# Layer norm 1 of two batches on a host-transposed x instead of TensorE transposes, and fc's first differences on VectorE

## The chip, the core and the metric

The kernel runs on one core of one Trainium2 chip, in float32 throughout. The metric is the device time of one execution in microseconds; the time before is given below as the median of three runs. The engines are named as in the profile: PE is TensorE (PEld its weight loads), DVE is VectorE, ACT is ScalarE, POOL is GpSimd and SP is SyncE, which here only issues DMAs.

## The reference

One block of cross-attention with an MLP. Four batches of 512 rows (queries) by 512 features, an encoder sequence of 512 rows per batch, 16 heads of 32, an MLP of 2048:

```python
x = layer_norm(hidden_states, ln1_w, ln1_b)          # (x - mu) * rsqrt(var + eps) * w + b
q = heads(x @ q_w + q_b)
k = heads(encoder_hidden_states @ k_w + k_b)
v = heads(encoder_hidden_states @ v_w + v_b)
attn = softmax(where(mask, q @ k.T * scale, min))
hidden = merge(attn @ v) @ cproj_w + cproj_b + hidden_states
y = layer_norm(hidden, ln2_w, ln2_b)
y = gelu(y @ fc_w + fc_b, approximate=True)
out = hidden + y @ proj_w + proj_b
```

Layer norm 1 takes a mean and a variance per row of x, and a weight and an offset per feature.

## The kernel before, in words

The tiles are 128 partitions by 512. A *window* w (16 of them) is one batch with four heads; a *block* is half a window, 256 queries, so there are 32 blocks p = 2w + half. Of a block the scores are made on PE into the eight PSUM banks (`scores`, L260), DVE adds the mask and finds the minimum (`soften`, L266), ACT takes the exponential (L270), DVE transposes 32x32 squares into a buffer tb (`turn`, L278), and `copies` (L327 to L340) brings the squares to the partitions where they are wanted: four copies on POOL and twelve DMAs on SP, into a buffer pT (or, for some pairs, gt or xe). `attend` (L343) multiplies with v on PE some two or three blocks later (the table `due`, L1021) and DVE writes the result (oT, L362). pT is a single buffer, so the copies of the next pair start when `attend` of the pair before has given it back.

Beside the blocks run the other products. `put(p, ...)` (L960) lists by hand what is emitted in block p; `block` emits it at three places, `fill(0)`, `fill(1)` and `fill(2)`, and `run` takes items off the list by their cost in the first two (CHAIN is 3.4, a work item of 0.0 costs nothing). There is no scheduler behind this: every engine and the SP queue works in the order in which instructions are emitted. PSUM banks are handed out in a ring of eight by `acc_tile`.

Layer norm 1 before: `ln_stat` takes the statistics of 128 rows on DVE, `ln_rs` turns them into a factor on POOL, `ln_norm` normalizes rows (ACT for batches 1 and 2, DVE for the others), and `ln1_turn` (L189, through `ln_turn`, L153) transposes on PE, four 128x128 transposes per group of 128 features, so 16 per batch, and applies weight and offset while it takes the result out of PSUM into xT, a half of the buffer xe. `prep_q` (L212 and after) reads xT; `prep_k` and `prep_v` read eT, the transposed encoder rows, which the host has already transposed (`encT`). For batch 1 x is loaded into gt at the start (L896), the norm is in block 0 and the turns in block 4. For batch 3 x is loaded in block 12, the statistics are in blocks 13 and 15, the norm in 15 and the turns in 16 and 17.

The MLP of batches 0 and 1 also runs beside the blocks. Its first product (`fc_by_pair`, `fc_seven`) uses Strassen-Winograd sums, seven products in place of eight: the four differences of the normalized rows are made once per batch by `y_sums` (L489), the sums of weights by `fc_sums` (L551) on POOL. For batches 0 and 1 two of the four differences are on DVE and two on POOL. For batch 0 that is in block 11, ahead of the first fc product.

DMAs of weights (`load_w`, `load_mlp`), of the encoder rows (`load_enc`) and of residual rows (`load_h`) share the SP queue with the twelve DMAs of each `copies`.

Of the kernel before, what the change touches and what calls it, by code (L numbers as in the profile page):

```python
# [35 lines left out]
IN_G = (1, 3, 5, 7)  # L36
IN_XE = (25, 27, 29, 31)

BY_ACT = ((1, 1), (1, 2))
NORM_ACT = BY_ACT + ((2, 0), (2, 1))  # L40
MW = 8
WARM = 9
# [5 lines left out]


@with_exitstack  # L50
def xattn_block(ctx: ExitStack, tc: tile.TileContext, x, encT, mask, q_w, k_w, v_w, c_w, fc_w, p_w, vecs, rows, out):
    nc = tc.nc
    scale = float(np.float32(1.0) / np.sqrt(HD).astype(np.float32))

    def pools(stack, **bufs):
        return [stack.enter_context(tc.tile_pool(name=n, bufs=k)) for n, k in bufs.items()]

    const, keep, hids, tiles, small = pools(ctx, const=1, keep=1, hids=6, tiles=4, small=4)
    dram = ctx.enter_context(tc.tile_pool(name="dram", bufs=1, space=bass.MemoryType.DRAM))

    att = ctx.enter_context(ExitStack())
# [6 lines left out]
    row = const.tile([P, 3, D], F32, tag="row", name="row")  # L68
    m8 = one.tile([P, L], U8, tag="m8", name="m8")
    nhalf = const.tile([P, NT], F32, tag="nhalf", name="nhalf")  # L70
    qb = const.tile([P, NG], F32, tag="qb", name="qb")
    wc = one.tile([P, ND, D], F32, tag="wc", name="wc")

# [56 lines left out]
    def ln_rs(key):  # L130

        ve = small.tile([P, NT], F32, tag="ve", name=f"ve{key[0]}_{key[1]}")
        nc.gpsimd.tensor_scalar(ve, S["mv", key][:, :, 1], EPS, 1.0, ALU.add, ALU.mult)
        rs = small.tile([P, NT], F32, tag="rs", name=f"rs{key[0]}_{key[1]}")
        nc.gpsimd.tensor_tensor(rs, ve, nhalf, ALU.pow)
        S["rs", key] = rs
        if key in NORM_ACT:
            nm = small.tile([P, NT], F32, tag="nm", name=f"nm{key[0]}_{key[1]}")
            nc.gpsimd.tensor_tensor(nm, S["mv", key][:, :, 0], rs, ALU.mult)
            nc.gpsimd.tensor_scalar(nm, nm, -1.0, 0.0, ALU.mult, ALU.add)  # L140
            S["nm", key] = nm
# [27 lines left out]
    def load_enc(b):  # L169
        for d in range(ND):  # L170
            queue(b).dma_start(out=eT[:, d, :], in_=encT[b, ts(d, P), :])
# [6 lines left out]
    def ln1(b, part):  # L178

        xn = S["xn", b]  # L180
        for t in range(NT):
            if part == 2:
                ln_norm((1, b), t, xn[t], xn[t])
            elif t // 2 == part:
                ln_stat((1, b), t, xn[t])
        if part == 1:
            ln_rs((1, b))

    def ln1_turn(b, d):  # L189
        ln_turn((1, b), d, S["xn", b], xT)  # L190
# [71 lines left out]
    def soften(w, qt, *heads):  # L262
        for h in heads:
            s = score_tile()
            mn = small.tile([P, 1], F32, tag="mn", bufs=2 * HG, name=f"mn_{w}_{qt}_{h}")
            nc.vector.tensor_tensor_reduce(  # L266
                out=s, in0=S["sc", w, qt][h], in1=S["mb", w // NG], scale=1.0, scalar=FMAX,
                op0=ALU.add, op1=ALU.min, accum_out=mn,
            )
            nc.scalar.activation(s, s, AF.Exp, bias=mn, scale=-1.0, accum_out=S["sums", w][:, qt, h : h + 1])  # L270
            if h % 2:
                S["ps", w, qt, h // 2] = score_pair()
# [7 lines left out]
    def block(w, half, fill, pairs):  # L280

        q0, q1 = 2 * half, 2 * half + 1
        if half == 0:
            S["sums", w] = small.tile([P, NT, HG], F32, tag="sums", name=f"sums_{w}")
        tb = S["tb", w, half] = two.tile([P, NI, PW + 2 * HD], F32, tag="tb", name=f"tb_{w}_{half}")
        scores(w, q0)
        scores(w, q1)
        soften(w, q0, 0, 1, 2, 3)
        soften(w, q1, 0, 1)
        turn(w, q0, 0)  # L290
        turn(w, q0, 1)
        soften(w, q1, 2, 3)
# [9 lines left out]
        nc.vector.transpose(  # L302
            tb[:, :, PW:].rearrange("p j (a q) -> p a j q", a=2), rr.rearrange("p a h d -> p (a h d)")
        )
# [65 lines left out]
    def stays(b, t):  # L370

        return b == 0 or b == SPLIT and t < 2

    def load_h(b, *ts_):

        if ("xa", b) not in S:
            S["xa", b] = dram.tile([L, D], F32, tag=f"xa{b}", name=f"xa{b}")
        for t in ts_:
            if b == B - 1:

                S["h", b, t] = k_q(t // 2, t % 2)
            else:
                pool, tag = (hids, "hid") if stays(b, t) else (tiles, "xn")
                S["h", b, t] = pool.tile([P, D], F32, tag=tag, name=f"h_{b}_{t}")
# [103 lines left out]

    def y_sums(b):  # L489
        y11, y12, y21, y22 = y_blocks(b)  # L490
        e = nc.vector if b > SPLIT else nc.gpsimd
        sub(ys[:, 0], y12, y11)
        sub(ys[:, 1], y22, ys[:, 0])
        sub(y12, y22, y12, e)
        sub(ys[:, 2], y21, ys[:, 1], e)
# [348 lines left out]
    def do(fn):  # L844
        return [(0.0, fn)]

    def A(w):
        if w >= NW:
            return []
        return [  # L850
            (CHAIN, lambda: prep_k(w)),
            (CHAIN, lambda: prep_q(w)),
            (CHAIN, lambda: prep_v(w)),
        ]
# [4 lines left out]
    def turns1(b):  # L859
        return [(TURN, lambda d=d: ln1_turn(b, d)) for d in range(ND)]  # L860
# [19 lines left out]
    nc.scalar.dma_start(out=vec, in_=vecs)  # L880
    make_identity(nc, ident)
    nc.gpsimd.memset(nhalf, -0.5)
    load_enc(0)
    load_w(0, nc.sync, ("wv",))
    load_x(0)
# [15 lines left out]
    prep_v(0)  # L901
    prep_k(1)
    run(turns1(0))
    load_h(0, *range(NT))
    nc.sync.dma_start(out=wc, in_=c_w)
    load_mlp()
# [4 lines left out]
    ln_rs((1, 1))  # L911
    prep_q(0)
    v_bias(0)

    def norm1(b, *ts_):
        for t in ts_:
            S["xn", b][t] = tiles.tile([P, D], F32, tag="xn", name=f"xn1_{b}_{t}")
            ln_norm((1, b), t, S["xn", b][t], gt[:, ts(t, D)])

    S["xn", 1] = [None] * NT  # L920
    x3 = turns1(1)
# [24 lines left out]
    def pb_(b):  # L946
        return do(lambda: proj_bias(b))
# [7 lines left out]
    def norm(b, *ts_):  # L955
        return do(lambda: [norm2(b, t) for t in ts_])

    ahead, fills = {}, {}

    def put(p, *work, before=()):  # L960

        work = [item for part in work for item in part]
        ahead[p] = list(before)
        fills[p] = work

    k2, q2, v2 = A(2)
# [1 line left out]
    k4, q4, v4 = A(4)  # L968
    k5, q5, v5 = A(5)
    k6, q6, v6 = A(6)  # L970
    put(0, [(CHAIN, lambda: prep_v(1)), v2, k2], do(lambda: norm1(1, *range(NT))))
    put(1, [k3, (0.0, lambda: prep_q(1)), (CHAIN, lambda: (prep_v(3), load_enc(1)))])
    put(2, [q2], [k4])
    put(3, [q3, v4])
    put(4, [k5], x3, [v5])
    put(5, [q4, q5])
    put(6, [k6, q6])
    x1, x2, x3, x4 = inputs(2)
# [44 lines left out]
    for p in range(2 * NW):  # L1023
        w, half = divmod(p, 2)
        if half == 0 and w and w % NG == 0:
            make_mb(w // NG)
        run(ahead[p])
        for pair in due.get(p, ()):
            attend(*divmod(pair, 2))

        def fill(n, work=fills[p]):
            if n or not work or work[0][0] <= CHAIN:
                run(work, CHAIN if n < 2 else None)

        block(w, half, fill, any(cost > CHAIN for cost, _ in fills[p]))

    gelus()
    first_c = FIRST * FQ // 2
# [59 lines left out]
```

## Time and profile before

| | |
|---|---|
| time, median of 3 runs | 768.9 us (768.01 to 770.72) |
| the profiled execution | 768.29 us, its span 766.5 us |
| PE busy | 760.6 us (99% of the span) |
| DVE, ACT, POOL busy | 594.7, 337.1, 312.6 us |
| PE transposes, 128 in all (L158) | 1.9% of the chain that ended last |
| DMA | 131.44 MB, mean 171 GB/s |

Times in the lines of the timeline and of the chain are microseconds from the start of the span, then the duration. In the timeline a bracket at the end of a line tells how long the engine had been idle and what ended that. The chain follows back from the last instruction, at each step to what released it, so its pieces add up to the span. The PE spends the whole attention stage, to about 510 us, and the MLPs behind it without a visible gap; each piece of the chain is then a product by its line.

### The profile page before, as it was taken

The numbers are of one execution on the slowest core, as the hardware profiler recorded it, in microseconds if no ns is written. First come the engines' busy times: TensorE is split into PE (matmuls) and PEld (weight loads), VectorE is DVE, ScalarE is ACT, GpSimd is POOL, SyncE is SP. The second block draws the span as 40 slices with busy tenths as digits, with TensorE's granted clock in tenths as the row PEclk, the third lists the DMA queues.
The fourth block names the chain that finished last, engine by engine and source line by source line (L and its number), as shares of the span: only waits on it lengthen the run. The fifth ranks groups of instructions, "written<-read, shape, count | busy, mean of one in ns | idle before, by whom it ended". The sixth has DMA issues, their size and how long they took to land.

```text
span 766.5 us, 13025 instructions
## 1 busy us (share of the span) xinstructions
PE 760.6 (99%) x4474; PEld 520.1 (68%) x4474; DVE 594.7 (78%) x1188; ACT 337.1 (44%) x761; POOL 312.6 (41%) x330
## 2 busy tenths in 40 slices
PE   9999999999999999999999999999999999999998
PEld 7656555566754745565554566447888889988997
DVE  3889899878989757887888989855777886747862
ACT  2676766564776444737753567501202221021200
POOL 1525447369466374234575444530060014303152
PEclk9999999999999999999999999999999999999999
DMA  9978788466866766675656866793724412146001
GB/s 330 319 223 228 180 209 253 117 196 193 254 196 189 189 208 180 163 185 130 173 128 190 214 197 193 173 296 132 262 101 129 162 34 90 35 131 219 2 15 42
DMA packets 58721, 131.44 MB, mean 171 GB/s; under 512 B 10992, under 2 KB 16752, under 8 KB 58528
## 3 DMA queue, kind: packets, MB, share of 16 engines
q1 hardware_dynamic: 56592, 123.58, 56.2%
q0 software_dynamic: 1920, 7.01, 2.7%
q8 instruction: 36, 0.59, 0.3%
q14 instruction: 29, 0.24, 0.1%
q10 hardware_dynamic: 144, 0.02, 0.0%
HBM read 66.08 MB, written 11.01 MB: 101 GB/s over the span
## 4 chain that ended last, share of the span: by engine, by line
PE 98%; DVE 1%; POOL 0%; ACT 0%; issue 0%; POOLq 0%
PE q L518 25%; PE accp L578 11%; PE r L665 8%; PE sc L260 8%; PE av L357 8%; PE accq L229 7%; PE accc L397 7%; PE accv L240 7%; PE acck L217 7%; PE q4p L701 2%; PE q1p L719 2%; PE tp L158 2%; PE warm L891 1%; DVE ptt L266 0%; PE q3p L701 0%; PE q5p L701 0%
## 5 line engine op out<-in xcount | busy, mean ns | idle before, releaser
L270 ACT ACTIVATE ptt<-ptt,mn 128x512 f32<-128x512 f32 x256 | 181.6, 711 | 148.6 <-DVE mn L266 148.6
L266 DVE CUSTOM_DVE_ANT_0 ptt<-sc,mb 128x512 f32<-128x512 f32 x256 | 160.5, 682 | 19.2 <-PE sc L260 19.2
L278 DVE STREAM_TRANSPOSE tb<-ptt 128x1024 f32<-128x1024 f32 x128 | 153.5, 1217 | 0.3 <-ACT ptt L270 0.2
L335 POOL COPY pT<-tb 32x1088 f32<-32x1088 f32 x96 | 105.2, 1096 | 38.1 <-DVE oT L362 14.4
L578 PE MATMUL accp<-pbt,gt 128*128 128x512 f32 x192 | 84.9, 596 | 0.0
L518 PE MATMUL q<-yT,gt 128*128 128x256 f32 x320 | 78.9, 380 | 0.0
L539 ACT ACTIVATE ga<-ga,vec 128x512 f32<-128x512 f32 x40 | 26.7, 714 | 92.0 <-DVE ga L472 92.0
L578 PEld LDWEIGHTS accp<-pbt,gt 128*128 128x128 f32 x192 | 35.9, 190 | 45.8 <-issue 39.3
L518 PEld LDWEIGHTS q<-yT,gt 128*128 128x128 f32 x320 | 60.9, 190 | 8.6 <-DMA xa<-pbt 0.2
L260 PE MATMUL sc<-pbt 32*128 32x512 f32 x512 | 64.7, 614 | 0.0
L240 PEld LDWEIGHTS accv<-ptt,xe 128*128 128x128 f32 x512 | 59.1, 192 | 7.4 <-DVE mn L266 4.9
L518 PE MATMUL q<-ys,gt 128*128 128x256 f32 x240 | 61.6, 380 | 0.0
L240 PE MATMUL accv<-ptt,xe 128*128 128x128 f32 x512 | 60.0, 276 | 0.0
L217 PE MATMUL acck<-xe,ptt 128*128 128x512 f32 x128 | 58.9, 603 | 0.0
L229 PE MATMUL accq<-xe,ptt 128*128 128x512 f32 (+1 forms) x136 | 58.3, 574 | 0.0
L397 PE MATMUL accc<-wc,oT 128*128 128x512 f32 x128 | 56.4, 597 | 0.0
L472 DVE TENSOR_TENSOR ga<-q,ga 128x512 f32<-128x512 f32 (+1 forms) x60 | 36.2, 603 | 21.4 <-PE q L518 19.4
L518 PEld LDWEIGHTS q<-ys,gt 128*128 128x128 f32 x240 | 45.7, 190 | 6.1
L270 ACT ACTIVATION_READ_ACCUMULATOR ptt<-ptt,mn 128x1 f32 x256 | 47.8, 187 | 0.0
L252 POOL TENSOR_TENSOR v<-v,row 128x512 f32<-128x512 f32 x16 | 20.4, 1280 | 64.7 <-ACT v L245 64.3
L357 PE MATMUL av<-pT,v 128*32 128x256 f32 x768 | 46.4, 382 | 0.0
L229 PEld LDWEIGHTS accq<-xe,ptt 128*128 128x128 f32 x136 | 25.1, 190 | 30.7 <-issue 23.1
(181 smaller groups left out, 1163.4 us busy)
## 6 DMA issues: line engine op xcount, KB each, us to landing
pT<-tb SPq DMA_DIRECT2D x288, 136.0 KB, 2.4
pbt<-p_w_dram SPq DMA_DIRECT2D x40, 256.0 KB, 3.3
gt<-ws SPq DMA_DIRECT2D x20, 512.0 KB, 3.4
gt<-tb SPq DMA_DIRECT2D x48, 136.0 KB, 2.4
xe<-tb SPq DMA_DIRECT2D x48, 136.0 KB, 2.4
pbt<-fc_w_dram SPq DMA_DIRECT2D x24, 256.0 KB, 4.1
gt<-fc_w_dram SPq DMA_DIRECT2D x20, 256.0 KB, 3.4
ptt<-k_w_dram SPq DMA_DIRECT2D x16, 256.0 KB, 3.7
```

The lines of the kernel that those rows point to most:

```text
L217: nc.tensor.matmul(acc, S["wk", w][:, d, :], eT[:, d, :], start=(d == 0), stop=(d == ND - 1))
L229: nc.tensor.matmul(acc, S["wq", w][:, d, :], xT[:, d, c], start=(d == 0), stop=(d == ND - 1))
L240: nc.tensor.matmul(acc[:, ts(t, P)], eT[:, d, ts(t, P)], S["wv", w][:, d, :], start=(d == 0), stop=(d == ND - 1),)
L260: nc.tensor.matmul(S["sc", w, qt][h], qT[r, ts(qt, P)], kT[r, :], start=True, stop=True)
L266: nc.vector.tensor_tensor_reduce(out=s, in0=S["sc", w, qt][h], in1=S["mb", w // NG], scale=1.0, scalar=FMAX, op0=ALU.add, op1=ALU.min, acc ...
L270: nc.scalar.activation(s, s, AF.Exp, bias=mn, scale=-1.0, accum_out=S["sums", w][:, qt, h : h + 1])
L278: nc.vector.transpose(tv[:, qt % 2, 2 * k : 2 * k + 2], S["ps", w, qt, k])
L335: nc.gpsimd.tensor_copy(pT[ts(i, HD), i], tb[ts(i, HD), i])
L357: nc.tensor.matmul(av[ts(h, HD), : 2 * P].rearrange(shape, **kw), v[:, t, ts(h, HD)], p[t][h], start=(t == 0), stop=(t == NT - 1),)
L397: nc.tensor.matmul(acc, S["oT", b][:, g, ts(t, P)], wc[:, g, :], start=(g == 0), stop=(g == NG - 1))
L518: nc.tensor.matmul(o, x[:, k], y[:, k], start=(k == 0), stop=(k == 1))
L578: nc.tensor.matmul(acc, gT[q % 2][:, k, ts(t, P)], S["pw", b, q * FQ + k], start=(k == 0), stop=(k == FQ - 1))
```

## The change

The host passes x a second time, transposed (`rawT`). For batches 1 and 3 (`BY_ROW`) the turn on PE is gone:

- `ln_rs` writes the factor and the negated mean times the factor, per row, into a small tile rn; `store_rn` transposes it on DVE and stores it to DRAM with four small DMAs, `load_rn` reads it back as two tiles in which each of 128 partitions holds all 512 rows' values.
- `load_raw` loads the transposed x (four tiles), `ln1_rows` multiplies and adds on POOL, two operations per tile, eight per batch, and `ln1_affine` applies weight and offset per feature on ACT, four operations, straight into xT.
- The row-wise norms, four per batch, and the 16 PE transposes of each of the two batches with their way out of PSUM are gone.
- In batch 1 `load_raw` is at the start, right behind the turns of batch 0 and ahead of `load_h`, `store_rn` in block 0, `load_rn` in block 1 behind the encoder's rows of the next batch, `ln1_rows` in blocks 2 and 3, `ln1_affine` in block 4. In batch 3 the statistics are all in block 13, `load_raw` in 13, `store_rn` and `load_rn` in 14, `ln1_rows` in 16, `ln1_affine` in 17.
- The residual tiles of batch 1 that stay in SBUF use the two buffers (tag hid2) that the spread rows had; `load_h(1, 0, 1)` moves from block 16 to 17.
- `y_sums` of batch 0 is wholly on DVE and moves from the first fill of block 11 to a new place `mid`, in the middle of the block's `soften`; for batch 1 it is as before.

```diff
-BY_ACT = ((1, 1), (1, 2))
+BY_ROW = ((1, 1), (1, 3))
+BY_ACT = ((1, 2),)
...
-    const, keep, hids, tiles, small = pools(ctx, const=1, keep=1, hids=6, tiles=4, small=4)
+    const, keep, hids, tiles, small = pools(ctx, const=1, keep=1, hids=4, tiles=4, small=4)
...
+        if key in BY_ROW:
+            rs, nm = rn[:, :NT], rn[:, NT : 2 * NT]
+            nc.gpsimd.tensor_tensor(rs, ve, nhalf, ALU.pow)
+            nc.gpsimd.tensor_tensor(nm, S["mv", key][:, :, 0], rs, ALU.mult)
+            nc.gpsimd.tensor_scalar(nm, nm, -1.0, 0.0, ALU.mult, ALU.add)
+            return
...
+    def load_raw(b):
+        S["xn", b] = [tiles.tile([P, L], F32, tag="xn", name=f"raw_{b}_{d}") for d in range(ND)]
+        for d in range(ND):
+            nc.sync.dma_start(out=S["xn", b][d], in_=rawT[b, ts(d, P), :])
+
+    def store_rn(b):
+        nc.vector.transpose(rnT, rn)
+        d = S["rn", b] = dram.tile([2, L], F32, tag=f"rn{b}", name=f"rn{b}")
+        for i in range(NI):
+            nc.sync.dma_start(
+                out=d.rearrange("a (t i q) -> i (a t) q", i=NI, q=HD)[i], in_=rnT[i * HD : i * HD + 2 * NT, :]
+            )
+
+    def load_rn(b):
+        S["rows", b] = [hids.tile([P, L], F32, tag="hid2", bufs=2, name=f"rn_{b}_{i}") for i in range(2)]
+        for i in range(2):
+            nc.sync.dma_start(out=S["rows", b][i], in_=S["rn", b][i : i + 1, :].broadcast_to([P, L]))
+
+    def ln1_rows(b, *ds):
+        for d in ds:
+            for i, op in enumerate((ALU.mult, ALU.add)):
+                nc.gpsimd.tensor_tensor(S["xn", b][d], S["xn", b][d], S["rows", b][i], op)
+
+    def ln1_affine(b):
+        for d in range(ND):
+            nc.scalar.activation(
+                xT[:, d, :], S["xn", b][d], AF.Identity,
+                bias=vec[:, LN1B + d : LN1B + d + 1], scale=vec[:, LN1W + d : LN1W + d + 1],
+            )
...
         soften(w, q0, 0, 1, 2, 3)
+        run(mid)
         soften(w, q1, 0, 1)
...
-        e = nc.vector if b > SPLIT else nc.gpsimd
+        e = nc.gpsimd if b == SPLIT else nc.vector
...
+    def next_(fn):
+        return [(0.01, fn)]
...
     run(turns1(0))
+    load_raw(1)
     load_h(0, *range(NT))
...
-    put(0, [(CHAIN, lambda: prep_v(1)), v2, k2], do(lambda: norm1(1, *range(NT))))
-    put(1, [k3, (0.0, lambda: prep_q(1)), (CHAIN, lambda: (prep_v(3), load_enc(1)))])
-    put(2, [q2], [k4])
-    put(3, [q3, v4])
-    put(4, [k5], x3, [v5])
+    put(0, [(CHAIN, lambda: prep_v(1)), v2], do(lambda: store_rn(1)), [k2])
+    put(1, [k3, (0.0, lambda: prep_q(1)), (CHAIN, lambda: (prep_v(3), load_enc(1), load_rn(1)))])
+    put(2, [q2], [k4], do(lambda: ln1_rows(1, 0, 1)))
+    put(3, [q3, v4], do(lambda: ln1_rows(1, 2, 3)))
+    put(4, [k5, v5], do(lambda: ln1_affine(1)))
...
-    put(11, [k], do(lambda: y_sums(0)), [v], some(2), pb_(0))
+    put(11, [k, v], some(2), pb_(0), mid=do(lambda: y_sums(0)))
...
-    put(13, [k], some(2), [v], x2[:1])
-    put(14, [q], some(2))
-    put(15, some(2), x2[1:2], some(1), x2[2:], some(1))
+    put(13, [k], x2[:1], some(2), [v], x2[1:2], do(lambda: load_raw(3)))
+    put(14, do(lambda: store_rn(3)), [q], do(lambda: load_rn(3)), some(2))
+    put(15, some(4))
...
-    put(16, h_(1, 0, 1), [k, q], x3[:2], some(2), x3[2:3])
-    put(17, [v], x3[3:], h_(1, 2, 3), x4, cb(1), C(1))
+    put(16, do(lambda: ln1_rows(3, *range(ND))), [k, q], some(2))
+    put(17, h_(1, 0, 1), [v], next_(lambda: ln1_affine(3)), h_(1, 2, 3), x4, cb(1), C(1))
```

More of the change, by code (lines that the diff above doesn't have):

```diff
@@ L50, in xattn_block @@
 @with_exitstack
-def xattn_block(ctx: ExitStack, tc: tile.TileContext, x, encT, mask, q_w, k_w, v_w, c_w, fc_w, p_w, vecs, rows, out):
+def xattn_block(ctx: ExitStack, tc: tile.TileContext, x, rawT, encT, mask, q_w, k_w, v_w, c_w, fc_w, p_w, vecs, rows, out):
     nc = tc.nc
@@ L70, in xattn_block @@
     nhalf = const.tile([P, NT], F32, tag="nhalf", name="nhalf")
+    rn, rnT = (const.tile([P, HD], F32, tag=n, name=n) for n in ("rn", "rnT"))
     qb = const.tile([P, NG], F32, tag="qb", name="qb")
@@ L278, in turn, with block @@
         nc.vector.transpose(tv[:, qt % 2, 2 * k : 2 * k + 2], S["ps", w, qt, k])
-    def block(w, half, fill, pairs):
+    def block(w, half, fill, pairs, mid):
         q0, q1 = 2 * half, 2 * half + 1
@@ L382, in load_h @@
             else:
-                pool, tag = (hids, "hid") if stays(b, t) else (tiles, "xn")
-                S["h", b, t] = pool.tile([P, D], F32, tag=tag, name=f"h_{b}_{t}")
+                pool, tag, n = (tiles, "xn", 4) if not stays(b, t) else (hids, "hid2", 2) if b else (hids, "hid", 4)
+                S["h", b, t] = pool.tile([P, D], F32, tag=tag, bufs=n, name=f"h_{b}_{t}")
             Q[0].dma_start(out=S["h", b, t], in_=x[b, ts(t, P), :])
@@ L882, in xattn_block @@
     nc.gpsimd.memset(nhalf, -0.5)
+    nc.gpsimd.memset(rn, 0.0)
     load_enc(0)
@@ L913, in xattn_block @@
     v_bias(0)
[L915 to L921, printed above, removed]
     mlp = [
@@ L956, in norm, with put @@
         return do(lambda: [norm2(b, t) for t in ts_])
-    ahead, fills = {}, {}
-    def put(p, *work, before=()):
+    ahead, mids, fills = {}, {}, {}
+    def put(p, *work, before=(), mid=()):
         work = [item for part in work for item in part]
-        ahead[p] = list(before)
+        ahead[p], mids[p] = list(before), list(mid)
         fills[p] = work
@@ L1033, in fill @@
                 run(work, CHAIN if n < 2 else None)
-        block(w, half, fill, any(cost > CHAIN for cost, _ in fills[p]))
+        block(w, half, fill, any(cost > CHAIN for cost, _ in fills[p]), mids[p])
     gelus()
@@ L1074 @@
         "x": a["x"],
+        "rawT": np.ascontiguousarray(a["x"].transpose(0, 2, 1)),
         "encT": np.ascontiguousarray(a["ctx_2048"].transpose(0, 2, 1)),
```

## The prediction, made before the changed kernel ran

> **What bounds the kernel now.** I read the head of the page first, then the waits of the PE, then the chain of waits, which tells what a microsecond is worth in each place.
>
> ```profile
> span 766.5 us, 13025 instructions
> PE 760.6 (99%) x4474; PEld 520.1 (68%) x4474; DVE 594.7 (78%) x1188; ACT 337.1 (44%) x761; POOL 312.6 (41%) x330
> ```
> ```profile
> PE q L518 <- POOL yT L469: 1.1, 1, 1.1
> ```
>
> The PE is busy in 99% of the span, and beside the start the list of its waits holds this one alone: 1.1 us in block 11, for a difference that `y_sums` makes on POOL. So PE work that goes is time won, and work on another engine costs nothing until it makes the PE wait. The questions are how much PE work goes, whether that one wait goes, and which slack the moved work uses up.
>
> **What goes from the PE.** Rows of the chain, in order of time:
>
> ```profile
> 74.27 1.75 PE tp L158 x16
> ...
> 252.21 0.87 PE tp L158 x8
> 253.08 6.05 PE q L518 x28
> 259.13 0.44 PE tp L158 x4
> ...
> 267.13 0.44 PE tp L158 x4
> ```
>
> The turns of batch 1 are 1.75 us on the chain, those of batch 3 0.87 + 0.44 + 0.44 = 1.75. All four pieces lie between PE products that follow at once, so the whole is won: **-3.50**. Their way out of PSUM and the eight row-wise norms go from ACT and DVE, which nobody waits for there: 0.
>
> **The wait in block 11.** Its timeline, PE and DVE:
>
> ```profile
> 171.38 0.69 DVE L469 TENSOR_TENSOR ys<-yT 128x512 f32<-128x512 f32 x1
> ...
> 172.10 1.89 PE L518 MATMUL q<-yT,pbt 128*128 128x256 f32 x8
> 172.10 1.46 DVE L469 TENSOR_TENSOR ys<-yT,ys 128x512 f32<-128x512 f32 x1
> ...
> 175.84 0.40 DVE L302 STREAM_TRANSPOSE tb<-rr 128x256 f32<-128x256 f32 x1
> ...
> 179.58 1.94 PE L357 MATMUL av<-pT,v 128*32 128x256 f32 x32
> 181.44 1.14 PE L260 MATMUL sc<-pbt 32*128 32x512 f32 x8
> ```
> ```profile
> L335 POOL COPY pT<-tb x4: 1082/1278/1509, 169.3 to 173.1; 32x1088 f32<-32x1088 f32 x4
> L472 DVE TENSOR_TENSOR ga<-q,ga 128x512 f32<-128x512 f32 (+1 forms) x60 | 36.2, 603 | 21.4 <-PE q L518 19.4
> ```
>
> The fc product takes 179.58 - 172.10 = 7.48 us here and 6.05 undisturbed (the chain's row at 253.08). If all four differences are there in time, 1.43 go: **-1.43**. They will be: before, the first two stood behind two transposes and all eight `soften` and began at 171.38; now they stand ahead of both transposes and of four `soften`, and their input, turned in block 10, has long been there.
>
> The price is on DVE. Two differences took 0.69 + 1.46 = 2.15 there; four take 4 x 0.69 = 2.76 if nothing holds them up. So the block's last transpose, which ended at 176.24, ends 0.6 later, and behind it stand four additions of 0.6 that empty fc's PSUM banks. They end near 176.24 + 0.6 + 2.4 = 179.2. The PE's next scores begin at 181.44 - 1.43 = 180.0 and reach fc's banks with their fifth head, halfway through them, about 1 us later. Slack 1.8.
>
> Why did one difference take 1.46 and the other 0.69? In the same microseconds a POOL copy took 1.51 where another took 1.08: the two hold each other up, by 0.77 for the DVE. How many of the four will meet a POOL operation I take as in the row, every second one: 1.5 us, which the slack just covers: **+0.1**, bounds 0 (none) and 1.3 (all four wait 0.77: 3.1 against 1.8).
>
> The Trainium skill, "SBUF — State Buffer", section "Who interferes with whom", states that a DVE instruction with two SBUF inputs and a POOL instruction that reads SBUF shut each other out, the later one for the whole of the other. The two long rows agree. Since POOL has sums of weights and copies queued at that time, by this rule every one of the four would wait, and the term would be its bound of 1.3; the fast row, 0.69 among the same copies, is why I don't take it.
>
> **Rows on POOL, eight operations per batch.** Nearest rows: the same shape and engine, SBUF in and out.
>
> ```profile
> L368 POOL TENSOR_TENSOR h<-h,row x18: 1260/1274/1460, 114.3 to 388.7; 128x512 f32<-128x512 f32 x18
> 261.98 0.72 POOL L472 TENSOR_TENSOR wsum<-pbt 128x256 f32<-128x256 f32 x1 [12.93 <-DMA pbt<-fc_w_dram]
> 266.39 4.49 POOL L335 COPY pT<-tb 32x1088 f32<-32x1088 f32 x4
> 281.30 1.86 PE av L357 x32
> ```
>
> Eight at 1.27 are 10.2 us. In block 16 POOL sits idle for 12.93 us up to 261.98, and the eight fall into that hole. What follows, the sums of weights, the copies of pair 16 (done at 270.88, wanted at 281.30), the bias of v and four `c_bias`, keeps its place. In blocks 2 and 3 four operations each, 5.1 us, lie ahead of copies that are wanted two to three blocks later. Cost **0**; without that cover each microsecond would be one on the PE (rival 3). The spread rows (four small stores, two loads back, through DRAM) are asked for a block ahead of `ln1_rows` in batch 1, two ahead in batch 3; on SP the copies of later pairs wait behind that round trip, with blocks to spare: 0.
>
> **ACT.**
>
> ```profile
> 78.75 2.78 ACT L163 ACTIVATE xe<-tp,vec 128x512 f32<-128x512 f32 x4
> 83.38 7.06 PE accq L229 x16
> ```
>
> In batch 1 four operations stay four, in batch 3 they are four for two. Behind the copy of v they begin about 79.4 and end 2.8 later, at 82.2; the PE wants the first tile at 83.38 - 1.75 = 81.6 and the fourth 2.6 us after that, at 84.2. **0**. In block 17 the residual loads `h_(1, 2, 3)` wait on the SP queue for the first two of these operations, and the encoder's rows of batch 3 wait behind them; both are read a good part of a block later: 0.
>
> **The start.** `load_raw(1)` puts 1.05 MB ahead of the residual rows, cproj's and the MLP's weights, and so ahead of the first copies and of batch 1's encoder rows, which the PE wants next.
>
> ```profile
> 41.19 1.03 SPq L210 DMA_DIRECT2D ptt<-k_w_dram  x2
> 47.27 1.85 SPq L171 DMA_DIRECT2D xe<-encT_dram  x4
> 52.42 3.43 PE acck L217 x8
> ```
> ```profile
> L171 SPq DMA_DIRECT2D xe<-encT_dram x1: 431/431/431, 48.7 to 48.7; - x1
> DMA to landing us min/median/max: 5.2/5.2/5.2
> 40.00:45.00 5.00, 5.00 (x25) 3.21 (x24) 4.83 (x9) 4.51 (x12) 0.00 (x0) 1.00 0.75 212
> 45.00:50.00 5.00, 5.00 (x36) 3.25 (x35) 2.98 (x9) 2.42 (x6) 2.34 (x3) 1.00 0.45 154
> ```
>
> Four such loads are 1.85 us of issue and, at the 212 GB/s of the row, up to 5.0 of transfer; four small stores add little. SP has next to nothing to issue from 42.2 to 47.27, and from 40 to 50 the DMA engines are idle for 5 x (0.25 + 0.55) = 4.0 us. The delay ends there, but for 1 us at most. The last encoder tile lands at 48.7 + 5.2 = 53.9; the PE reads it as the fourth of four, at 52.42 + 2.6 = 55.0. Slack 1.1. **0**, upper bound 1.6.
>
> **Pair 13.** Here the slack is smallest: `load_raw(3)` stands on the SP queue just ahead of this pair's twelve DMAs.
>
> ```profile
> 212.60 8.20 SPq L340 DMA_DIRECT2D pT<-tb  x12
> 223.55 1.93 PE L357 MATMUL av<-pT,v 128*32 128x256 f32 x32
> ```
> ```profile
> L340 SPq DMA_DIRECT2D pT<-tb x1: 589/589/589, 220.2 to 220.2; - x1
> DMA to landing us min/median/max: 3.1/3.1/3.1
> 210.00:212.00 2.00, 2.00 (x38) 0.99 (x36) 0.19 (x2) 1.79 (x2) 1.60 (x3) 1.00 0.34 121
> 212.00:214.00 2.00, 2.00 (x20) 0.91 (x18) 1.32 (x4) 0.24 (x2) 1.62 (x3) 1.00 0.18 45
> 214.00:216.00 2.00, 2.00 (x5) 0.94 (x6) 2.00 (x7) 2.00 (x7) 1.98 (x4) 1.00 1.02 301
> ```
>
> The last of the twelve lands at 220.2 + 3.1 = 223.3 and the PE wants it at 223.55. The raw tiles go from about 210.5 (the last one behind DVE's last statistics, about 212), when the DMA engines are at 0.34 and 0.18, which leaves 2.7 us of their time; 1.05 MB at 301 GB/s are 3.5. About 0.8 spill into the copies' time, less the slack of 0.25: **+0.6**, bounds 0 and 3.2 (nothing of it hidden).
>
> **Sum.** -3.50 - 1.43 + 0.1 + 0.6 = -4.23. The profiled execution took 768.29 (span 766.5 and 1.8 around it), so 764.1. The median of the three runs is 768.9, 0.6 above the profiled one; I say **764.3**, between the two. With the terms at their good ends it is 768.29 - 4.93 = 763.4, with the first and second of them at their bad ends 768.29 - 4.93 + 1.3 + 1.1 = 765.8 (1.1 of pair 13).
>
> **Rivals.**
> 1. Pair 13 is late by the whole 1.05 MB: +3.2 in place of +0.6, **766.9**. For it: the DMA share of 1.02 right afterwards. Against: the free engines before.
> 2. The wait of block 11 moves rather than goes: all four differences wait for POOL, the scores of block 12 for DVE, +1.3 in place of +0.1, **765.5**. For it: 1.46 beside 0.69. Against: the 0.69. By the section of the Trainium skill named above it would be this one.
> 3. Slower: the row operations on POOL. They have 12.93 us of hole and 281.30 - 1.75 - 270.88 = 8.7 of slack behind it, so from 21.6 us for the eight, 2.7 each, `attend` of pair 16 waits. To end 2.3 above the time before they must take 21.6 + 4.2 + 2.3 = 28 us, 3.5 each; at 4 us each the stall is 10.4 and the time **774.6**. For it: POOL is named in the only wait, and no row shows a spread row as second input. Against: 1.27 in 18 rows, 1.46 at most.
> 4. The encoder's rows are late at 52.42 by the bound: +1.6, **765.9**.
>
> **How the numbers follow.** The forecast 0.62, rival 1 0.12, rival 2 0.10, rival 3 0.09, rival 4 0.07. About 0.3%, 2.3 us, is what a measurement of this kernel can tell from no change, so faster begins below 766.0: the forecast, rival 2 and most of rival 4, 0.78. Same: rival 1 and the rest of 4, 0.13. Slower: rival 3, 0.09. The range reaches from 762.9 (the good ends, and half a microsecond that a lighter DVE and ACT may win) to 767.2, over rivals 1, 2 and 4. The forecast's own is 763.4 to 765.8.
>
> **What would show it.** Right: no tp rows of batches 1 and 3, their neighbours on the chain touching; no PE wait for L469 and an fc product of 6.05 in block 11; row operations of 1.27 on POOL; the PE's av of pair 13 starting 0 to 1 us late, behind a DMA. Wrong: a PE wait for xT (the first accq of a batch behind ACT), for encoder rows at 52, for copies that stand behind `ln1_rows` on POOL, or scores behind DVE in block 12.

## The result and the profile after

The changed kernel takes 767.2 us (median of 17 runs, 765.15 to 769.48) against 768.9 us of the kernel before (17 runs, 767.78 to 770.72). The ratio is 0.9981, its interval 0.9973 to 0.9988: a gain of about 1.5 us, a third of the forecast 4.6, and 767.23 lies just outside the predicted range, which ended at 767.2. The profiled execution took 767.06 us.

The head of the page and, from the waits, the lines of the PE beside the start (total us, times, longest):

```profile
span 764.9 us, 13013 instructions
PE 758.5 (99%) x4442; PEld 516.5 (68%) x4442; DVE 591.0 (77%) x1186; ACT 336.0 (44%) x759; POOL 329.2 (43%) x347
```
```profile
PE av L396 <- DMA rn<-rnT: 1.3, 1, 1.3
PE av L396 <- POOL pT L374: 0.4, 1, 0.4
```

The one wait of before, in block 11, is gone, and two have come, both ahead of an `attend`. A third does not look like a wait: it lies inside a product. The chain shows all three (start, us, engine and product):

```profile
69.23 2.84 PE sc L298 x16
72.08 3.63 PE acck L255 x8
75.71 3.57 PE accv L278 x32
79.28 1.86 PE av L396 x32
...
172.00 6.05 PE q L557 x28
...
189.66 1.09 POOL pT L374
...
191.94 1.93 PE av L396 x32
...
222.26 1.60 DMA rn<-rnT
223.86 1.92 PE av L396 x32
...
252.49 6.04 PE q L557 x28
258.54 1.86 PE av L396 x32
```

What was forecast as won is there: k, v and av of block 4 touch without turns between them, fc's product of block 11 takes 6.05, and the one at 252.49 is followed by av at once. But the scores of block 4 take 2.84 us where they take 1.93 elsewhere, POOL's copies stand ahead of pair 11's av, and a DMA ahead of pair 13's.

**A ledger.** The PE is nearly always busy, so the start of one product on the chain, minus its start in the first profile of before, is the time won or lost up to that place. Between two columns the difference is what the stretch has won (negative) or given back. The columns are the first v, then av of the pairs 0, 2, 10, 11, 13 and 16, named by their place in before (v at 9.23; av at 55.85, 79.59, 179.65, 193.12, 223.62 and 281.30), and the end of the span (766.5). Ahead of av 56 lies the k product with the last encoder tiles of batch 1; ahead of av 80 the scores of block 4 and batch 1's turns; ahead of av 180 the fc product of block 11; ahead of av 193 and av 224 what the copies of pairs 11 and 13 cost; ahead of av 281 batch 3's turns.

| kernel | v | av 56 | av 80 | av 180 | av 193 | av 224 | av 281 | end |
|---|---|---|---|---|---|---|---|---|
| before, again | -0.2 | -0.2 | -0.2 | -0.2 | -0.2 | -0.2 | -0.2 | -0.1 |
| before, third | 0.6 | 0.6 | 0.6 | 0.6 | 0.6 | 0.6 | 0.6 | 0.6 |
| after | 0.5 | 0.5 | -0.3 | -1.6 | -1.2 | 0.2 | -1.5 | -1.6 |
| after, again | -0.5 | -0.5 | -2.2 | -3.5 | -3.1 | -2.0 | -3.7 | -3.8 |
| after, third | 0.0 | 0.3 | -1.5 | -2.8 | -2.4 | -1.2 | -2.9 | -3.1 |
| after, fourth | 0.5 | 2.6 | 2.3 | 1.0 | 1.4 | 2.0 | 0.3 | 0.1 |

Behind its start, every profile of before keeps the same distance to the first one. After wins the turns (1.75 us in block 4 where nothing is in the way, 1.7 behind av 224) and 1.3 in block 11, each time, and 0.15 behind av 281: 4.9 in all. It gives back 0.4 at pair 11 and 0.6 to 1.4 at pair 13 each time, and in some executions up to 2.1 at the start (v to av 56) and up to 1.4 in block 4. Over the four, the mean of what is given back is 0.6 up to av 56, 0.6 in block 4, 0.4 at pair 11 and 1.1 at pair 13: 2.7 of the 4.9, which leaves 2.2. (The first v is 0.1 late in the mean, but so it is in the three of before.) The spans agree: 764.4 in the mean of the four and 766.7 in the mean of the three, 2.3 apart.

The times are only 1.9 apart, 766.6 and 768.5, and the medians of all runs on the two chips 1.7 and 1.3. The rest lies outside the span, where no row of the profile shows it: the time minus the span is 1.7 to 1.9 us in every run of before that has a span on record, and 2.1 to 2.2 in every run of after, 0.35 more. The kernel of run 8 below does not have it (1.7 to 1.8), that of run 9 has (2.1 to 2.2), and neither has the rows of batches 1 and 3; so the rows are not needed for it, and its cause stays open.

In the rows that follow, nothing was lost.

In the timelines of after, the four differences on DVE (start, us, line, operation), and on POOL what ran beside them and, later, the eight row operations:

```profile
166.40 0.93 DVE L508 TENSOR_TENSOR ys<-yT 128x512 f32<-128x512 f32 x1
167.44 1.03 DVE L508 TENSOR_TENSOR ys<-yT,ys 128x512 f32<-128x512 f32 x1
168.39 0.68 DVE L508 TENSOR_TENSOR yT<-yT 128x512 f32<-128x512 f32 x1
168.99 0.68 DVE L508 TENSOR_TENSOR ys<-yT,ys 128x512 f32<-128x512 f32 x1
```
```profile
166.86 1.05 POOL L508 TENSOR_TENSOR wsum<-pbt,wsum 128x256 f32<-128x256 f32 x1
168.21 0.56 POOL L600 DMA_DIRECT2D ws<-wsum  x1 [0.30 <-POOL wsum L508]
168.77 0.54 POOL L601 DMA_DIRECT2D ws<-pbt  x1
...
248.67 10.37 POOL L218 TENSOR_TENSOR raw<-raw,rn 128x512 f32<-128x512 f32 x8
```

The eight take 10.37 us, 1.30 each, in POOL's idle stretch of block 16, and no PE wait stands near them. Of the four differences two take 0.25 and 0.35 longer than 0.68. They lie over POOL's sum at 166.86, itself 1.05 where such sums take 0.73; the two short ones begin where POOL only issues DMAs.

### The profile page after: what moved, and what is told of

Read it like the earlier page. It is cut to its first block, busy times and chain, and to the rows that moved or that the text cites. A ratio compares the mean times of both kernels' runs of the same rounds, so it can differ in the third digit from the quotient of the medians.

```text
span 764.9 us, 13013 instructions
## 1 busy us (share of the span) xinstructions
PE 758.5 (99%) x4442; PEld 516.5 (68%) x4442; DVE 591.0 (77%) x1186; ACT 336.0 (44%) x759; POOL 329.2 (43%) x347
## 4 chain that ended last, share of the span: by engine, by line
PE 98%; DVE 1%; POOL 0%; issue 0%; DMA 0%; SPq 0%; POOLq 0%
PE q L557 24%; PE accp L617 11%; PE sc L298 8%; PE r L704 8%; PE av L396 8%; PE accv L278 8%; PE acck L255 8%; PE accc L436 7%; PE accq L267 7%; PE q4p L740 2%; PE q1p L758 2%; PE tp L166 1%; DVE ptt L304 1%; PE warm L934 1%; PE q3p L740 0%; PE q7p L740 0%
```

## The experiments

Theories. A: the time is given back at three places that each have one cause, and a move of that one thing takes the loss away (block 4: `load_rn(1)` ahead of pair 1's DMAs; pair 11: POOL's order; pair 13: `load_raw(3)`). B: the raw tiles and rows load DMA and POOL as a whole, so that a wait moved at one place comes back at the next. Times are medians; "-" lines are after's unless said otherwise.

**1. `load_rn(1)` behind pair 1's DMAs.**

```diff
-    put(1, [k3, (0.0, lambda: prep_q(1)), (CHAIN, lambda: (prep_v(3), load_enc(1), load_rn(1)))])
+    put(1, [k3, (0.0, lambda: prep_q(1)), (CHAIN, lambda: (prep_v(3), load_enc(1)))], next_(lambda: load_rn(1)))
```

> The changed kernel, but the spread rows of batch 1 are loaded behind pair 1's twelve DMAs in block 1 instead of ahead of them. Theory (the scores of block 4 were late because DVE's first transposes of block 3 waited for the buffer tb, which pair 1's DMAs still read): those DMAs end about 1 to 2 us earlier, DVE's idle 1.26 us ahead of the transposes of block 3 and most of the 0.92 us on the PE in block 4 go: 0.5 to 0.9 us less than the changed kernel. Rival (the 1 MB of raw rows at the start is what makes DMAs late): the wait stays, no difference over 0.2 us.

767.09 us, 0.9979 (0.9969 to 0.9988). The SP queue and DVE in before with the scores of block 4 on its chain, then the same two in after (its scores are in the chain above), then all three in this kernel:

```profile
49.21 7.81 SPq L340 DMA_DIRECT2D gt<-tb  x12
62.48 2.37 DVE L278 STREAM_TRANSPOSE tb<-ptt 128x1024 f32<-128x1024 f32 x2
68.71 1.93 PE sc L260 x16
```
```profile
49.68 1.08 SPq L213 DMA_DIRECT2D rn<-rn  x2
50.87 9.48 SPq L379 DMA_DIRECT2D gt<-tb  x12
...
64.34 2.37 DVE L316 STREAM_TRANSPOSE tb<-ptt 128x1024 f32<-128x1024 f32 x2 [1.26 <-ACT ptt L308]
```
```profile
51.25 7.80 SPq L379 DMA_DIRECT2D gt<-tb  x12
...
63.78 2.37 DVE L316 STREAM_TRANSPOSE tb<-ptt 128x1024 f32<-128x1024 f32 x2
```
```profile
70.02 1.93 PE sc L298 x16
```

In before the issue of pair 1's twelve DMAs began at 49.21 and took 7.81, to 57.02, which is 1.2 us behind av of pair 0 (55.85). In after it ends at 60.35, 4.0 behind (56.37), here at 59.05, 1.9 behind (57.16). Of after's twelve the last was issued at 59.8, and with their median of 4.1 us to landing that is 63.9. They read tb, which has two buffers, and the transposes at 64.34 write the same one again: DVE stands idle for 1.26 us, and the PE's scores of block 4 wait inside for banks that DVE has not emptied. With `load_rn(1)` behind, DVE doesn't stand idle, the scores take 1.93, and the stretch from av 56 to av 80 wins its whole 1.75 (1.31 to -0.44). The timeline names ACT as the releaser, though ACT's exponentials for these four heads had ended by 62.99 and DVE's idle time began only at 63.08: the name is of the semaphore that came last by the record, not of the cause.

One profile would not show this, since two of after's four lose nothing here either. But all five profiles with this move (runs 1, 4, 5, 6 and 14) win the whole 1.75 in block 4, and of the seven without it (after's four, runs 2, 3 and 7) five lose 0.85 to 1.4. The time does not show it: 0.5 to 0.9 less than after was expected, and the ratio is that of after. In this profile pair 13 gave back 2.3 and the start 1.4; what the other runs gave back there is not on record. A holds at this place by the profiles.

**2. `load_raw(3)` out of pair 13's way.**

```diff
-    put(13, [k], x2[:1], some(2), [v], x2[1:2], do(lambda: load_raw(3)))
+    put(13, [k], x2[:1], some(2), [v], x2[1:2])
-    put(15, some(4))
+    put(15, do(lambda: load_raw(3)), some(4))
```

> The changed kernel, but the raw rows of batch 3 are loaded in block 15 instead of 13; the four small stores stay in block 14. Theory (pair 13's DMAs stood behind 1 MB of raw rows): the PE's wait of 1.33 us ahead of pair 13 goes, 1.0 to 1.4 us less than the changed kernel unless pair 14 waits next (its copies on POOL ended 1.0 us before they were wanted). Rival (the small stores hold the semaphore or the queue, as the named releaser says): the wait of 1.3 us stays.

765.14 us, 0.9953 (0.9939 to 0.9967). The SP queue of after around pair 13's DMAs, then this kernel's, then its chain:

```profile
209.50 2.60 SPq L200 DMA_DIRECT2D raw<-rawT_dram  x4
212.22 9.47 SPq L379 DMA_DIRECT2D pT<-tb  x12
221.79 1.43 SPq L206 DMA_DIRECT2D rn<-rnT  x4
```
```profile
212.25 8.43 SPq L379 DMA_DIRECT2D pT<-tb  x12
220.79 1.45 SPq L206 DMA_DIRECT2D rn<-rnT  x4
```
```profile
217.23 6.04 PE q L557 x28
223.27 1.86 PE av L396 x32
```

The PE's av of pair 13 follows fc's product at once. Without the raw tiles the twelve are issued in 8.43 us in place of 9.47 (8.20 before), the last at 220.1 in place of 221.1, and their median way to landing is 3.3 us in place of 3.9, the longest 4.2 in place of 6.2. The small stores rn<-rnT, which the waits of after name, are still there: they stand behind the twelve on the queue and only land last. Nothing came back at block 14 or later (-0.35 at av 224, -2.11 at av 281, which is batch 3's turns). A holds again. The median is 2.1 us below after's, where the profiles of after show 1.1 for this place; the difference is not explained.

**3. The bias of the residual rows behind pair 11's copies.**

```diff
-    put(11, [k, v], some(2), pb_(0), mid=do(lambda: y_sums(0)))
+    put(11, [k, v], some(2), mid=do(lambda: y_sums(0)))
-    put(13, [k], x2[:1], some(2), [v], x2[1:2], do(lambda: load_raw(3)))
+    put(13, pb_(0), [k], x2[:1], some(2), [v], x2[1:2], do(lambda: load_raw(3)))
```

> The changed kernel, but the four POOL additions of proj's bias (5.0 us) move from block 11 to the start of block 13. Theory (pair 11's copies on POOL stand behind them and end 0.4 us late): the PE's 0.43 us of waiting for POOL's copy goes, 0.4 to 0.5 us less than the changed kernel. Rival (pair 11's DMAs are late as well): the wait stays, with a DMA as its releaser.

766.82 us, 0.9976 (0.9965 to 0.9987). POOL in before, in after and here:

```profile
187.65 4.47 POOL L335 COPY pT<-tb 32x1088 f32<-32x1088 f32 x4
```
```profile
176.82 1.27 POOL L290 TENSOR_TENSOR v<-v,row 128x512 f32<-128x512 f32 x1 [2.81 <-ACT v L283]
...
182.50 4.96 POOL L407 TENSOR_TENSOR h<-h,row 128x512 f32<-128x512 f32 x4
187.41 4.47 POOL L374 COPY pT<-tb 32x1088 f32<-32x1088 f32 x4
```
```profile
183.06 4.49 POOL L374 COPY pT<-tb 32x1088 f32<-32x1088 f32 x4
```

In before the copies of pair 11 ended at 192.12 and the PE wanted them at 193.05. After moves the PE up by 1.3 and POOL by 0.25 only. POOL has lost its two differences (2 x 1.27), but now stands idle for 2.81 us until ACT has copied v:

```profile
175.15 0.58 ACT L245 COPY v<-accv 128x512 f32<-128x512 f32 x1
```
```profile
173.80 0.72 ACT L308 ACTIVATE ptt<-ptt,mn 128x512 f32<-128x512 f32 x1 [1.97 <-DVE mn L304]
...
176.09 0.58 ACT L283 COPY v<-accv 128x512 f32<-128x512 f32 x1
```

The first row is before's, the others after's: the copy of v is 0.94 later, since ACT's exponentials ahead of it wait for DVE's `soften`, which the four differences in `mid` push back. So the copies end at 191.88, the PE's av starts at 191.94, and 0.4 of the 1.3 is gone again. With the bias behind, the copies end at 187.6 and the wait is gone (-0.99 at av 180, at av 193 and at av 210). It is gone in all five profiles with this move (runs 3, 4, 5, 6 and 14), and 0.4 stands there in all seven of after and its variants without it. A holds for the third time, and the loss belongs to the differences, not to the rows; run 8 shows it alone. The time cannot tell 0.4 us: the intervals of 0.9976 here and 0.9981 for after overlap.

**4 and 5. The three moves together.** Run 1's and run 3's edits, with `load_raw(3)` and `load_rn(3)` both in block 15 (run 2's move, and the loads of the rows with it). Run 5 is the same kernel once more, beside runs of after on the same chip.

```diff
-    put(13, [k], x2[:1], some(2), [v], x2[1:2], do(lambda: load_raw(3)))
-    put(14, do(lambda: store_rn(3)), [q], do(lambda: load_rn(3)), some(2))
-    put(15, some(4))
+    put(13, pb_(0), [k], x2[:1], some(2), [v], x2[1:2])
+    put(14, do(lambda: store_rn(3)), [q], some(2))
+    put(15, do(lambda: (load_raw(3), load_rn(3))), some(4))
```

> All three moves in one, and the spread rows of batch 3 loaded in block 15 too. Theory (three separate waits of 0.92, 0.43 and 1.33 us, each of one cause): together 2.0 to 2.7 us less than the changed kernel, about 764.5 us in the runs' median, 4.4 less than before. Rival (a new wait takes each place): no more than 1.2 us less than the changed kernel.

> The kernel with all three moves once more, beside the changed kernel on the same chip. Theory (three waits, one cause each): 1.5 to 2.5 us less than the changed kernel in the runs' median. Rival: less than 1 us.

765.42 us, 0.9963 (0.9950 to 0.9977), and again 765.09 us, 0.9952 (0.9940 to 0.9963), beside 767.63 of after on that chip: 2.5 us less than after, where 1.5 to 2.5 was expected. The chain of the second one:

```profile
48.01 7.47 DMA xe<-encT_dram
...
221.50 1.93 PE av L396 x32
```

| kernel | v | av 56 | av 80 | av 180 | av 193 | av 224 | av 281 | end |
|---|---|---|---|---|---|---|---|---|
| run 4 | 0.1 | 1.4 | -0.4 | -1.7 | -1.7 | -1.7 | -3.4 | -3.6 |
| run 5 | -0.7 | 0.8 | -1.0 | -2.2 | -2.2 | -2.1 | -3.8 | -4.0 |
| run 1 | -0.1 | 1.3 | -0.4 | -1.7 | -1.3 | 1.0 | -0.7 | -0.9 |
| run 2 | 0.7 | 1.3 | 0.4 | -0.8 | -0.4 | -0.4 | -2.1 | -2.3 |
| run 3 | -0.1 | 1.1 | 0.3 | -1.0 | -1.0 | 0.1 | -1.6 | -1.8 |

Behind av 56 the three moves win everything that was forecast as won: 1.75, 1.3, 0, 0.0 to 0.1 lost at pair 13, 1.7. In these two executions nothing has come back elsewhere, against B; runs 6 and 14, which hold the three moves too, do show new waits. What is left is the stretch ahead of av 56, the product with the last encoder tiles of batch 1: 1.2 and 1.5 given back in these two. In run 5 the wait has the name of the encoder's rows themselves. In run 4 it has that of DVE, but the first of the four tiles was issued at 47.75 and landed 5.4 us later, at 53.15, and the product began at 53.23.

By time alone the sum of the three is less clear than by the profiles: run 2, with one of the moves, took 765.14 on the chip on which run 4 took 765.42, six runs each.

**6 and 7. The MLP's weights out of the start.** They stand on the queue between the raw tiles and the encoder's rows; run 6 moves them in run 4's kernel, run 7 in after's.

```diff
-    load_mlp()
-    put(7, [v6, k], cb(0))
+    put(7, [v6, k], cb(0), do(load_mlp))
```

> The kernel with all three moves, and the first 2 MB of MLP weights loaded in block 7 instead of at the start. Theory (batch 1's encoder rows land late at 53 us because the raw rows are one load too many for the DMA engines of the first 50 us): the PE's 0.7 us of waiting ahead of k of block 2, and the 1.2 us that this stretch lost in all, go; 1.0 to 1.3 us less than with the three moves alone, 4.6 less than before. Rival (the wait is for DVE, as the named releaser says): it stays.

> The changed kernel with nothing but the first 2 MB of MLP weights moved to block 7. Theory (a full DMA queue at the start makes both the encoder rows and pair 1's DMAs late): no wait ahead of k in block 2, and the 0.92 us of block 4 go as well, though the spread rows are still loaded ahead of pair 1's DMAs; pair 11 and pair 13 keep theirs: 0.9 to 1.5 us less than the changed kernel. Rival (the place of the spread rows alone holds up pair 1's DMAs): block 4 keeps its 0.9 us.

765.41 us, 0.9962 (0.9950 to 0.9974), and 767.12 us, 0.9978 (0.9967 to 0.9989): no gain over run 4 and after, where about 1 us was expected. Ahead of av 56 the two give back 0.4 and 0.1, less than most others, but run 6 has a new wait at pair 13. Its POOL, PE and weight loads:

```profile
210.18 0.73 POOL L511 TENSOR_TENSOR wsum<-pbt 128x256 f32<-128x256 f32 x1 [7.47 <-DMA pbt<-fc_w_dram]
...
217.93 4.47 POOL L374 COPY pT<-tb 32x1088 f32<-32x1088 f32 x4
```
```profile
222.45 1.93 PE L396 MATMUL av<-pT,v 128*32 128x256 f32 x32 [1.62 <-DMA ptt<-q_w_dram]
```
```profile
222.45 1.45 PEld L396 LDWEIGHTS av<-pT,v 128*32 128x32 f32 x32 [2.02 <-POOL pT L374]
```

POOL's sums wait for weights until 210.18, its copies of pair 13 end at 222.40, and the PE starts at 222.45. The matmuls' row names a DMA, but the weight loads of the same product name the copy. In run 7 block 4 still gave back 1.4, as it may with `load_rn(1)` where it was (the rival's forecast), pair 13 1.85, and 0.5 came at a place of block 8.

**8 and 9. The differences alone.** Run 8 is before with the differences on DVE in `mid`, without the rows; run 9 is before with the first two lines of this edit only: on DVE, where they were.

```diff
-        e = nc.vector if b > SPLIT else nc.gpsimd
+        e = nc.gpsimd if b == SPLIT else nc.vector
...
+        run(mid)
...
-    put(11, [k], do(lambda: y_sums(0)), [v], some(2), pb_(0))
+    put(11, [k, v], some(2), pb_(0), mid=do(lambda: y_sums(0)))
```

> The kernel before with the second part of the change alone: all four differences of batch 0 on VectorE, in the middle of block 11's row minima. Theory: the fc product of block 11 takes 6.05 us instead of 7.48, and pair 11's copies on POOL, which follow ACT's later copy of v, take back 0.4 to 0.5 at the start of block 13: 0.9 to 1.0 us less than before. Rival (the late copies of pair 11 come from the raw rows' part): the whole 1.43 us stay won.

> The kernel before with all four differences on VectorE at their old place, behind all row minima of block 11. Theory (the engine was the matter, not the place): VectorE's four take 2.8 to 4 us from 171.4, the last ends at 174.2 to 175.4, ahead of the product that reads it; the fc product takes 6.05 to 6.4 us, and ACT's copy of v is late by as much as with the new place, so 0.6 to 1.2 us less than before. Rival (the place is what does it): the fc product still waits 0.5 us or more.

768.13 us, 0.9986 (0.9977 to 0.9995), and 769.11 us, 1.0005 (0.9997 to 1.0014). The chain of run 8, and then POOL and the weight loads of av in run 9:

```profile
190.94 1.09 POOL pT L336
```
```profile
188.01 4.47 POOL L335 COPY pT<-tb 32x1088 f32<-32x1088 f32 x4
```
```profile
192.53 1.45 PEld L357 LDWEIGHTS av<-pT,v 128*32 128x32 f32 x32 [1.18 <-POOL pT L335]
```

| kernel | v | av 56 | av 80 | av 180 | av 193 | av 224 | av 281 | end |
|---|---|---|---|---|---|---|---|---|
| run 6 | -0.4 | 0.1 | -1.7 | -2.8 | -2.8 | -1.2 | -2.9 | -3.0 |
| run 7 | 0.5 | 0.6 | 0.2 | -0.5 | -0.1 | 1.7 | 0.0 | -0.1 |
| run 8 | 0.4 | 1.0 | 1.0 | -0.3 | 0.1 | 0.2 | 0.2 | 0.2 |
| run 9 | -0.6 | -0.5 | -0.5 | -1.4 | -0.6 | -0.5 | -0.5 | -0.5 |

Run 8 has no rows, wins 1.34 in block 11 and gives 0.4 back at pair 11 as after does. So that loss is the differences' own. In run 9 the engine alone wins 0.8, and pair 11 takes all of it: POOL's copies end at 192.48, av starts at 192.53. A gain of 0.6 to 1.2 was expected of run 9, and none came: the median of its eleven spans is 766.9, as in before on that chip, and the time outside the span is 0.35 longer. (That its profiled span ends 0.5 early is the start's, -0.6 at the first v.) What the differences' new place wins over the old one is 0.5 in fc's product and 0.35 at pair 11. Run 8 also gave back 0.66 ahead of av 56, without a raw tile or a row in it.

**10 to 13. Before and after, two more profiles of each.** No edit.

> The kernel before, unchanged, for a second profile. Theory (k of block 2 waits for encoder rows in every kernel of this family, by as much as the DMAs happen to be late, and the changed kernel's raw rows add to it): a wait ahead of k in block 2 of 0 to 0.7 us, none in block 4, none at pairs 11 and 13. Rival (the wait belongs to the raw rows alone): none.

> The kernel before, unchanged, for a third profile; as with the second: 0 to 0.7 us ahead of k in block 2 by the theory, none by the rival.

> The changed kernel, unchanged, for a second profile. Theory: waits of 0.8 to 1.0 us in block 4, 0.4 to 0.5 at pair 11 and 1.1 to 2.3 at pair 13 in every execution, and 0.5 to 1.4 us ahead of k in block 2 whenever the first k of the kernel is not late. Rival (the first profile was a chance): one or more of the four is missing.

> The changed kernel, unchanged, for a third profile; as with the second: waits in block 4, at pair 11 and at pair 13 by the theory, one or more of them missing by the rival.

768.12, 768.99, 764.83 and 765.58 us. They are the rows of the first ledger: pairs 11 and 13 give back in every profile of after, the stretch ahead of av 56 and block 4 in some. Before gives back nothing at any of the four places, so the theory that it too waits ahead of av 56 is not borne out.

**14 and 15. The raw tiles of batch 1 behind pair 1's DMAs, and after once more.** Run 14 is run 4's kernel without raw tiles at the start; the eight row operations move to block 3.

```diff
-    load_raw(1)
-    put(1, [k3, (0.0, lambda: prep_q(1)), (CHAIN, lambda: (prep_v(3), load_enc(1)))], next_(lambda: load_rn(1)))
-    put(2, [q2], [k4], do(lambda: ln1_rows(1, 0, 1)))
-    put(3, [q3, v4], do(lambda: ln1_rows(1, 2, 3)))
+    put(1, [k3, (0.0, lambda: prep_q(1)), (CHAIN, lambda: (prep_v(3), load_enc(1)))],
+        next_(lambda: (load_raw(1), load_rn(1))))
+    put(2, [q2], [k4])
+    put(3, do(lambda: ln1_rows(1, 0, 1, 2, 3)), [q3, v4])
```

> The kernel with all three moves, and the raw rows of batch 1 loaded behind pair 1's DMAs in block 1, together with the spread rows; all eight POOL operations of batch 1 in block 3. Theory (the raw rows at the start make batch 1's encoder rows late): no wait ahead of k in block 2 beyond what the kernel before has, 0.4 to 1.2 us less than with the three moves alone. Rival (that wait is the DMA's scatter and not the raw rows): as long as with the three moves alone, within 0.3 us.

> The changed kernel once more, on the same chip as the two others. Theory: 0.2 to 0.3% less than before, with the waits at pair 11 (0.5 us) and pair 13 (1.1 to 1.4 us) and, in some executions, in block 4 (0.9).

765.32 us, 0.9951 (0.9938 to 0.9964), no different from run 5's 765.09 on the same chip, and 767.63 us, 0.9983 (0.9971 to 0.9995), for after. The first line is from run 14's waits of the PE; then DVE and the chain, and then the weight loads of pair 13's av:

```profile
PE acck L255 <- DMA xe<-encT_dram: 1.6, 2, 0.9
```
```profile
76.64 2.37 DVE L316 STREAM_TRANSPOSE tb<-ptt 128x1024 f32<-128x1024 f32 x2 [0.77 <-DMA pT<-tb]
...
82.02 2.35 PE sc L298 x15
```
```profile
223.82 1.24 PEld L396 LDWEIGHTS av<-pT,v 128*32 128x32 f32 x28 [0.65 <-POOL pT L374]
```

| kernel | v | av 56 | av 80 | av 180 | av 193 | av 224 | av 281 | end |
|---|---|---|---|---|---|---|---|---|
| run 14 | 0.6 | 2.3 | 0.6 | -0.3 | -0.3 | 0.2 | -1.5 | -1.6 |

It gives back 1.7 ahead of av 56 without a raw tile on the queue before it; the fourth profile of after gave back 2.1 with them. So the raw tiles at the start are not shown to be the cause. The weight loads show that the product waits for the encoder's tiles: for 3.1 us here, 1.4 in the fourth of after, 2.3 in run 8, and not at all in the three of before and in run 9. Why these tiles land late stays open; nine of the twelve profiles with rows give back 0.3 or more there.

Two more waits are new here. The raw tiles and the rows now stand ahead of pair 2's DMAs, DVE stands idle for them at 76.64, the DMAs' own name beside it, and the scores of the next block take 2.35: run 1's loss, one pair later. And POOL, whose sums waited for weights until 211.54, ends its copies of pair 13 at 223.77, with 0.5 lost, as in run 6. So A holds for its three places, but B is not refuted: these two profiles show that a load moved to another place can make a wait there.

## Why the prediction was wrong, by its steps

- **Turns, -3.50: right.** 1.75 in block 4 where nothing is in the way, 1.7 in blocks 16 and 17 in all profiles.
- **Block 11, -1.43: right in mechanism**, 1.3 in the ledger, the product 6.05. **The hold-up, +0.1:** nothing was lost: two of four were held up as assumed, but by 0.25 and 0.35 rather than 0.77 each, and no scores stood behind DVE in block 12. The Trainium skill, "SBUF — State Buffer", section "Who interferes with whom", fits these rows better than the prediction had it: the two differences that met a POOL sum on SBUF were long, the two beside POOL's DMA issues were not. The error was to take a POOL with work queued for a POOL that computes all the time. The fast row of before, 0.69, was also misread as an exception: it began at 171.38, ahead of the POOL copy that began at 171.5, and that copy was the one with 1.51; the difference behind it began during the copy and took 1.46. The later one paid each time.
- **The step that is missing at pair 11: failed, +0.4.** The prediction followed the later DVE only to fc's banks. It also delays `soften`, so ACT's exponentials, so ACT's copy of v, which POOL needs before it comes to pair 11's copies; and these had 0.93 us to spare before, less than the 1.3 by which the PE moved up in block 11. Runs 3 and 8 show it.
- **"On SP the copies of later pairs wait behind that round trip, with blocks to spare: 0": failed, +0.6.** It asked when pT is wanted by the PE and forgot who waits for tb to be read: two buffers, so the pair after next waits on DVE, and behind it the PE's scores. Run 1 shows it for `load_rn(1)`. It is not in every execution of after.
- **Pair 13, +0.6: mis-sized.** 0.6 to 1.4 in four profiles, 1.1 in the mean, 2.3 in run 1; the mechanism is right (run 2). The bound of 3.2 held; the slack of 0.25 and the bytes alone did not give the size, since the landing of the twelve also got longer.
- **The start, 0 with a bound of 1.6: mis-sized.** 0.6 up to av 56 in the mean, 2.1 once, over the bound. Rival 4's place was right; that the raw tiles cause it is not shown, since run 14 has the wait without them.
- **"Span 766.5 and 1.8 around it": failed, +0.35.** The sum kept the 1.8 for the changed kernel without a reason, and it is 2.1 to 2.2. Why stays open.
- **Rows on POOL, 0, and ACT, 0: right.** 10.37 us in the idle stretch against 10.2, no wait. Rival 3 fell, and so did rival 2, since no scores of block 12 waited.

In sum: 4.9 won as forecast; 2.7 given back inside the span and 0.35 outside it, where the forecast had 0.7. Of the 2.3 missed, 1.35 (0.4, 0.6 and 0.35) are three steps with no price, and most of the rest is two prices too low, the start by 0.6 and pair 13 by about 0.5. That 767.23 nearly touches the range is chance: its upper end stood for rivals 1, 2 and 4, and none of them came as it was priced.

## What to carry to other kernels

On a kernel whose main engine is never idle, a microsecond won there makes all others late by a microsecond from that place on: list, for each consumer behind it, how long its input had been ready in the profile before, and any slack below the gain is a loss. When a load is put ahead of a buffer's DMAs, ask for both ends of that buffer: who waits for what it writes, and who waits to overwrite what it reads. Three moves in the order of emission, found so, took 765.1 us against 767.6 of the kernel after and 769.0 of the kernel before, all on one chip. Ask also what a moved load now stands ahead of: in run 14 the raw tiles and rows, put behind one pair's DMAs, stood in the way of the next pair's.

## What the runs showed of the hardware

DMA times differ between executions of one kernel by more than the terms argued about: the product with the last encoder tile of batch 1 lost between 0 and 2.1 us in four executions of after. The start differs too, the first v from 0.5 us early to 0.5 late in these four, and that is not the DMAs alone: of the first k product, weight loads that follow each other by 0.43 us in the second profile of before come 0.86 apart in the third, up to 7.07 us, with "issue" beside them and a granted clock of 1.0. The first profile of after alone would have put 0.9 us on block 4 and nothing on the stretch ahead of av 56; the third has 0.3 there and nothing in block 4. A POOL sum of 0.73 us took 1.05 under a DVE difference, and the differences 0.93 and 1.03 in place of 0.68: both pay.
